# Spectral convolution in a graph layer: complex products combined when they leave the bank, and an inverse transform on full tiles of 128 rows

## The chip, the core and the metric

The kernel runs on one core of one Trainium2 chip. The metric is the device time of one execution in microseconds. In the profile PE is TensorE (matmuls), PEld its weight loads, DVE is VectorE, ACT is ScalarE, POOL is GpSimd and SP is SyncE, which issues transfers. All data is fp32.

## What is computed

One layer of a graph network on 32 sequences of 512 tokens with 256 channels. Cut to what matters:

```python
h = relu(layernorm(x))                                  # (32, 512, 256)
xc = transpose(h)                                       # channels first
c = relu(bn1(conv1d(xc, conv1_w, pad=0)))               # 1 tap
c = bn2(conv1d(c, conv2_w, pad=8))                      # 17 taps, 256 -> 256 channels
x_conv = transpose(relu(c + xc))
s = h @ w_se.T + b_se                                   # 3 features a token
A = exp(-squared_distances(s)) * adj                    # (512, 512) for each sequence
x_nmp = A @ relu(h @ w_msg.T + b_msg)
gi = concat(x_conv, x_nmp) @ w_ih.T + b_ih              # gates of a GRU cell
gh = h @ w_hh.T + b_hh
r, z = sigmoid(gi_r + gh_r), sigmoid(gi_z + gh_z)
out = x + (1 - z) * tanh(gi_n + r * gh_n) + z * h
```

## The kernel before

The 17-tap convolution is done by a discrete Fourier transform. A sequence is cut into 8 pieces of 64 tokens; each piece and the taps are transformed at length 80, which gives 40 units: unit 0 holds the two real frequencies, the units 1 to 39 one complex frequency each. In each unit the spectra of 128 pieces (16 sequences, one half of the batch) are multiplied with the 256 x 256 weights of that frequency. A complex product is put together from three real ones (re and im are the spectra, wr and wi the weights):

- k1 = re (wr + wi)
- k2 = (re + im) wi
- k3 = (im - re) wr
- real part = k1 - k2, imaginary part = k1 + k3

The kernel before never forms the last line. It writes k1, k2 and k3, and the inverse transform has three rows per unit whose coefficients hold the sums. So a piece of tokens has 3 x 40 = 120 rows.

The stages, in order of time: transform of the first 16 sequences, and of the taps (up to about 165 us); "nodes", the aggregation A @ messages, with the products of the first half between (to about 455); transform of the second half, with the last products of the first half and sums of gate weights between (to about 590); nodes and products of the second half (to about 890); then the gates, two sequences (a "pair") at a time, each pair with its inverse transform (to the end).

```python
UNITS = L // 2                                 # L = 80, V = 64 tokens in a piece
ROWS = 3 * UNITS
...
back[3::3], back[4::3], back[5::3] = 2 * (cos - sin).T, -2 * cos.T, -2 * sin.T
...
def product(pw, g, u, xf):                     # half g of the batch, unit u
    ...
    y = pw.tile([P, 3, D], FP, tag="y", name=f"y_{g}_{u}", bufs=3)
    p = bank(f"py_{g}_{u}")                    # one of 8 PSUM banks, in turn
    if u == 0:
        terms = [(p[:, :D], re, wr), (p[:, D : 2 * D], im, wi)]
    else:
        both, wsum = BOTH.pop((g, u)), WSUM.pop((g, u))
        p2 = bank(f"py2_{g}_{u}")
        terms = [(p2[:, :D], both[:, 1], wr), (p[:, D : 2 * D], both[:, 0], wi), (p[:, :D], re, wsum)]
    for dst, v, w in terms:
        for ic in range(DC):
            nc.tensor.matmul(dst, v[:, ic, :], w[:, ic, :], start=(ic == 0), stop=(ic == DC - 1))     # L381
    for k in range(2):
        nc.scalar.copy(by_half(y[:, k, :]), halves(p[:, k * D : (k + 1) * D]))                        # L383
    if u == 0:
        nc.vector.memset(y[:, 2, :], 0.0)
    else:
        nc.vector.tensor_copy(by_half(y[:, 2, :]), halves(p2[:, :D]))                                 # L387
    nc.scalar.dma_start(YD[g][:, 3 * u : 3 * u + 3, :], y)                                            # L388
...
def combine_weights():                         # sums of gate weights, between the second half's transforms
    for k, src in enumerate((w_hhT, w_ihT[D:], w_ihT[:D])):
        w, t = (pools["sums"].tile([P, n, 3 * P], FP, tag=f"w{n}", ...) for n in (4, 7))   # one buffer each
        ...                                    # load w; 4 steps on GpSimd and ScalarE (L825), then write t out
...
def load_pair(p, queue=nc.sync):
    yt = [pools["ops"].tile([ROWS, W // 2, D], FP, tag="yt", ..., bufs=5) for k in range(4)]
    ...
    queue.dma_start(t, YD[g][w : w + W // 2].rearrange("w r d -> r w d"))                             # L535
...
def inverse(p):                                # W = 8 pieces, DC = 2 halves of the channels
    CP[p] = pools["ops"].tile([P, 7, N], FP, tag="cp", name=f"cp_{p}")
    for j in range(2):
        for oc in range(DC):
            bk = bank(f"pc2_{2 * p + j}_{oc}")
            for w in range(W):
                t0, t1 = max(0, w * V - PAD), min(N, w * V - PAD + L)
                u0 = t0 - (w * V - PAD)
                nc.tensor.matmul(bk[:, t0:t1], YT[p][j * W + w][:, oc * P : (oc + 1) * P],
                                 back[:, u0 : u0 + t1 - t0], start=(w == 0), stop=(w == W - 1), ...)  # L572
            xc = CP[p][:, 2 * oc + j, :]
            nc.vector.scalar_tensor_tensor(xc, bk, scale2[:, oc : oc + 1], HP[p][:, 2 * oc + j, :],
                                           op0=ALU.mult, op1=ALU.add)                                 # L575
            nc.scalar.activation(xc, xc, AF.Relu, bias=shift2[:, oc : oc + 1], scale=1.0)             # L577
...
for p in range(pairs):                         # the last stage
    ...
    gates_rz(p, terms, between)                # PE pg, L583
    inverse(p + 1)                             # PE pc, L572
    sums(CP[p + 1], False)                     # GpSimd, L561: four differences of the seven operands
    gate_n(p, terms, False)                    # PE pn, L583
```

The gates multiply 2 x 2 blocks with seven products in place of eight, so each operand (HP, NP, CP) has four blocks and differences of them. In the transform stages a sequence needs: statistics on VectorE (L282, L284, L287), 1/std on GpSimd (L288), normalising on VectorE (L294), transposes on TensorE (phT, L305), the 1-tap convolution (pc, L318) and the transform (px, L333).

Of the kernel before, what the change touches and what calls it, by code (L numbers as in the profile page):

```python
# [11 lines left out]
FP = mybir.dt.float32  # L12
# [3 lines left out]
P = 128  # L16
# [11 lines left out]
ROWS = 3 * UNITS  # L28
WROWS = 2 * UNITS


def dft_constants(taps):

    u = np.arange(L)[:, None]
    f = np.arange(1, UNITS)[None, :]
    cos, sin = np.cos(2 * np.pi * u * f / L), np.sin(2 * np.pi * u * f / L)
    alt = (1.0 - 2.0 * (np.arange(L) % 2))[:, None]
    spectrum = np.zeros((L, L))
    spectrum[:, :1], spectrum[:, 1:2] = 1.0, alt
    spectrum[:, 2::2], spectrum[:, 3::2] = cos, -sin  # L40
    forward = np.zeros((2 * V, 2 * L))
    forward[:V, :L] = forward[V:, L:] = spectrum[:V]
    weights = np.zeros((L, WROWS))
    weights[:, :1], weights[:, 1:2] = 1.0, alt
    weights[:, 2::2], weights[:, 3::2] = cos, -sin

    back = np.zeros((ROWS, L))
    back[0], back[1] = 1.0, alt[:, 0]
    back[3::3], back[4::3], back[5::3] = 2 * (cos - sin).T, -2 * cos.T, -2 * sin.T

    groups = np.zeros((P, WROWS))
    for q in range(4):
        groups[32 * q : 32 * q + taps] = weights[:taps][::-1]
    return [a.astype(np.float32) for a in (forward, groups, back / L)]
# [3 lines left out]
def gnn_layer(  # L58
# [59 lines left out]
    fwd_np, taps_np, back_np = dft_constants(KT)  # L118
# [4 lines left out]
    w1_in = early.tile([P, DC, D], FP, name="w1_in")  # L123
    load_rows(w1_in, w1T, nc.scalar)
    fwd = early.tile([P, 2 * L], FP, name="fwd")
    nc.scalar.dma_start(fwd, nc.inline_tensor(fwd_np, name="dft_fwd").ap())
    taps = early.tile([P, WROWS], FP, name="taps")
    nc.scalar.dma_start(taps, nc.inline_tensor(taps_np, name="dft_taps").ap())
    back = consts.tile([ROWS, L], FP, name="back")
# [43 lines left out]
    batch_norm("bn1", scale1, shift1, nc.gpsimd)  # L173
# [4 lines left out]
    setup = ExitStack()  # L178
    pools["setup"] = setup.enter_context(tc.tile_pool(name="setup", bufs=2))
    ones = pools["setup"].tile([P, P], FP, name="ones", bufs=1)  # L180
    nc.vector.memset(ones, 1.0)

    def bn1_row(i, v):
        for c in range(DC):
            diag = pools["setup"].tile([P, P], FP, tag="diag", name=f"diag_{i}_{c}")
            nc.scalar.activation(diag, ident, AF.Copy, scale=v[:, c : c + 1])
            nc.tensor.matmul(row1[i][:, c * P : (c + 1) * P], ones, diag, start=True, stop=True)

    def scale_w1():
        for c in range(DC):  # L190
            nc.vector.tensor_mul(w1[:, c, :].rearrange("p (i q) -> p i q", i=DC), by_parity(w1_in[:, c, :]),
                                 by_parity(row1[0][:, :D]))
# [3 lines left out]

    bn1_row(0, scale1)
    bn1_row(1, shift1)
    setup.close()

# [24 lines left out]
    WD = dram.tile([WROWS, D * D + 4 * D], FP, name="wd")  # L225
# [18 lines left out]
    def weights_to_freq(gen, pc, i):  # L244

        per = N // D
        s = i % SI
        if s == 0:
            for q in range(4):
                WST[q] = gen.tile([WROWS, SI, D], FP, tag="wst", name=f"wst_{pc}_{i}_{q}", bufs=8)  # L250
        ps = []
        for q in range(4):
            p = bank(f"pw_{pc}_{i}_{q}")
            nc.tensor.matmul(p[:WROWS, :], taps[32 * q : 32 * q + KT, :],  # L254
                             W2P[pc][32 * q : 32 * q + KT, i : i + per, :], start=True, stop=True)
            ps.append(p)
        for q in range(4):
            dst = WST[q][:, s : s + per, :]
            src = ps[q][:WROWS, :].rearrange("r (i d) -> r i d", d=D)
            if q == 3 or (q == 1 and s == 0):  # L260
                nc.vector.tensor_copy(dst, src)
            else:
                nc.scalar.copy(dst, src)
        if s + per == SI:
            for q in range(4):
                i0 = QI * q + PI * pc + i + per - SI
                nc.sync.dma_start(WD[:, i0 * D : (i0 + SI) * D], WST[q].rearrange("r i d -> r (i d)"))

# [96 lines left out]
    def product(pw, g, u, xf):  # L365
        if u > 0 and (g, u) not in BOTH or (g, u) not in WT:
            prepare(pw, g, u, xf)
        wt = WT.pop((g, u))
        re, im = factors_of(xf, u)
        wr, wi = wt[:, 0], wt[:, 1]  # L370
        y = pw.tile([P, 3, D], FP, tag="y", name=f"y_{g}_{u}", bufs=3)
        p = bank(f"py_{g}_{u}")
        if u == 0:
            terms = [(p[:, :D], re, wr), (p[:, D : 2 * D], im, wi)]
        else:
            both, wsum = BOTH.pop((g, u)), WSUM.pop((g, u))
            p2 = bank(f"py2_{g}_{u}")
            terms = [(p2[:, :D], both[:, 1], wr), (p[:, D : 2 * D], both[:, 0], wi), (p[:, :D], re, wsum)]
        for dst, v, w in terms:
            for ic in range(DC):  # L380
                nc.tensor.matmul(dst, v[:, ic, :], w[:, ic, :], start=(ic == 0), stop=(ic == DC - 1))  # L381
        for k in range(2):
            nc.scalar.copy(by_half(y[:, k, :]), halves(p[:, k * D : (k + 1) * D]))  # L383
        if u == 0:
            nc.vector.memset(y[:, 2, :], 0.0)
        else:
            nc.vector.tensor_copy(by_half(y[:, 2, :]), halves(p2[:, :D]))  # L387
        nc.scalar.dma_start(YD[g][:, 3 * u : 3 * u + 3, :], y)  # L388
# [104 lines left out]
    def combine_weights():  # L493

        steps = []
        for k, src in enumerate((w_hhT, w_ihT[D:], w_ihT[:D])):
            w, t = (pools["sums"].tile([P, n, 3 * P], FP, tag=f"w{n}", name=f"w{n}_{k}") for n in (4, 7))
# [25 lines left out]
    def load_pair(p, queue=nc.sync):  # L523
        yt = [pools["ops"].tile([ROWS, W // 2, D], FP, tag="yt", name=f"yt_{p}_{k}", bufs=5) for k in range(4)]
        HP[p] = pools["ops"].tile([P, 8, N], FP, tag="hp", name=f"hp_{p}")
        NP[p] = pools["ops"].tile([P, 7, N], FP, tag="np", name=f"np_{p}")
        YT[p] = []
        for j in range(2):
            b = 2 * p + j
            queue.dma_start(HP[p][:, j:4:2], HD[b])  # L530
            g, w0 = b // GB, (b % GB) * W
            for k in range(2):
                t = yt[2 * j + k]
                w = w0 + k * (W // 2)
                queue.dma_start(t, YD[g][w : w + W // 2].rearrange("w r d -> r w d"))  # L535
                YT[p] += [t[:, i, :] for i in range(W // 2)]
# [26 lines left out]
    def inverse(p):  # L563

        CP[p] = pools["ops"].tile([P, 7, N], FP, tag="cp", name=f"cp_{p}")
        for j in range(2):
            for oc in range(DC):
                bk = bank(f"pc2_{2 * p + j}_{oc}")
                for w in range(W):
                    t0, t1 = max(0, w * V - PAD), min(N, w * V - PAD + L)  # L570
                    u0 = t0 - (w * V - PAD)
                    nc.tensor.matmul(bk[:, t0:t1], YT[p][j * W + w][:, oc * P : (oc + 1) * P], back[:, u0 : u0 + t1 - t0],  # L572
                                     start=(w == 0), stop=(w == W - 1), skip_group_check=True)
# [203 lines left out]
    def first_part(g, freq, between, left=()):  # L777
# [3 lines left out]
        for b in range(b0, b0 + 3):  # L781
            if b not in X:
                load_x(b, nc.gpsimd if g else nc.sync)
# [59 lines left out]
    with tc.tile_pool(name="freq", bufs=1) as fpool:  # L843
# [3 lines left out]
        with phase("first", "gen"):  # L847
            gen = pools["gen"]
            per = N // D
            steps = [partial(weights_to_freq, gen, pc, i) for pc in range(QI // PI) for i in range(0, PI, per)]  # L850
            load_x(0)
# [68 lines left out]


# [88 lines left out]
```

## Time and profile before

| | |
|---|---|
| time | 1888.97 us, median of 3 (1886.87 to 1891.18) |
| span of the profiled execution | 1883.5 us |
| matmul records of the inverse transform (L572) | 1024, in 16 groups of 64 |
| granted TensorE clock, mean | 0.994 |
| transfers | 309.89 MB, mean 165 GB/s |
| write of a unit's products (yd) | 80 times 384 KB |
| read of a part of a sequence's products (yt) | 480 KB, four per pair |

An fp32 matmul stands in the trace as two records (a pass each). A row of the groups reads: line, engine, operation, what is written from what, shape and count; then busy time in us and the mean of one in ns; then the idle time of the engine ahead of them and what ended it. The mean of one matmul record is longer than the spacing of two, as matmuls overlap; what a matmul costs in a stream is read from a stretch without gaps, divided by its records. The chain of waits gives, followed back from the end, what each moment of the span was spent on.

### The profile page before, as it was taken

The page shows a single profiled execution, that of the slowest core. Times are in us where ns is not written, and L with a number is a line of the kernel's source. Part 1 is how long each engine was busy: PE and PEld are TensorE (multiplying, and loading weights), DVE is VectorE, ACT ScalarE, POOL GpSimd, SP SyncE. Part 2 cuts the span into 40 slices and gives each one's busy share as a digit, 9 for nine tenths or more (in the row PEclk, how much of TensorE's full clock was granted, in tenths as well). Part 3 has the DMA queues.
Part 4 walks back from the last instruction along what each step waited for, and adds up shares of the span by engine and source line. Part 5 has one row for each costly group of instructions (what it writes and reads, how often), then busy time and mean ns, then how long its engine had stood idle before and what let it go on. Part 6 is the DMA issues. An engine that isn't in the chain of part 4 may idle for free.

```text
span 1883.5 us, 20947 instructions
## 1 busy us (share of the span) xinstructions
PE 1844.1 (98%) x6982; PEld 1110.4 (59%) x6982; DVE 1084.0 (58%) x2162; ACT 599.9 (32%) x1153; POOL 583.1 (31%) x565
## 2 busy tenths in 40 slices
PE   7999999999999999999999999999999999999997
PEld 5677666665888676665545554555445554555453
DVE  7775554544986445444266456654665456645666
ACT  3545443432335444343212221222212221222121
POOL 3331343434432344445321332133222322133220
PEclk9999999999999999999999999999999999999999
DMA  7999998776568997878542455235532554245512
GB/s 217 292 273 236 252 265 250 217 221 208 173 235 206 263 273 240 249 226 230 146 103 57 104 132 131 59 73 131 132 81 53 129 132 106 55 102 131 131 28 40
DMA packets 316537, 309.89 MB, mean 165 GB/s; under 512 B 148631, under 2 KB 245815, under 8 KB 316047
## 3 DMA queue, kind: packets, MB, share of 16 engines
q1 hardware_dynamic: 289727, 232.09, 48.4%
q10 hardware_dynamic: 19024, 49.17, 7.2%
q0 software_dynamic: 7680, 27.30, 5.3%
q8 instruction: 56, 0.92, 0.2%
q14 instruction: 50, 0.41, 0.1%
HBM read 201.60 MB, written 106.89 MB: 164 GB/s over the span
## 4 chain that ended last, share of the span: by engine, by line
PE 91%; issue 2%; DVE 2%; DMA 2%; POOL 1%; ACT 1%; SPq 0%; POOLq 0%; ACTq 0%; DVEq 0%
PE pg L583 29%; PE pn L583 14%; PE pn L474 11%; PE py L381 11%; PE pc L572 6%; PE pm L425 6%; PE pc L318 5%; PE px L333 3%; PE pw L254 2%; PE pd L460 2%; PE phT L305 1%; PE psr L449 1%; DMA hT<-hd 1%; DVE stats L282 0%; PE pz L583 0%
## 5 line engine op out<-in xcount | busy, mean ns | idle before, releaser
L561 POOL TENSOR_TENSOR hp<-hp 128x512 f32<-128x512 f32 x64 | 94.8, 1491 | 467.2 <-DMA hp<-hd 366.9
L474 PE MATMUL pn<-A,msg 128*128 128x512 f32 x512 | 225.0, 592 | 0.0
L583 PE MATMUL pg<-hp,sw 128*128 128x512 f32 x434 | 221.9, 593 | 0.7 <-DVE rz L602 0.5
L583 PE MATMUL pg<-cp,sw 128*128 128x512 f32 x434 | 221.6, 592 | 0.0
L583 PE MATMUL pg<-np,sw 128*128 128x512 f32 x434 | 221.6, 592 | 0.0
L474 PEld LDWEIGHTS pn<-A,msg 128*128 128x128 f32 x512 | 97.1, 190 | 110.6 <-issue 107.7
L362 POOL TENSOR_TENSOR both<-xf 128x256 f32<-128x256 f32 x78 | 60.3, 773 | 321.4 <-PE py L381 288.7
L381 PE MATMUL py<-wt,both 128*128 128x256 f32 x624 | 150.4, 384 | 0.7 <-issue 0.7
L598 ACT ACTIVATE rz<-rz,brz 128x512 f32<-128x512 f32 x93 | 67.0, 721 | 260.2 <-DVE rz L602 260.2
L583 PEld LDWEIGHTS pg<-hp,sw 128*128 128x128 f32 x434 | 82.2, 190 | 104.8 <-issue 97.6
L583 PEld LDWEIGHTS pg<-cp,sw 128*128 128x128 f32 x434 | 82.5, 190 | 103.8 <-issue 103.8
L583 PEld LDWEIGHTS pg<-np,sw 128*128 128x128 f32 x434 | 82.5, 190 | 103.8 <-issue 103.8
L381 PEld LDWEIGHTS py<-wt,both 128*128 128x128 f32 x624 | 114.1, 190 | 43.4 <-issue 26.5
L466 DVE TENSOR_TENSOR A<-e,at 128x512 f32<-128x512 f32 x128 | 111.5, 910 | 41.7 <-ACT e L463 41.6
L561 POOL TENSOR_TENSOR cp<-cp 128x512 f32<-128x512 f32 x64 | 80.5, 1268 | 177.2 <-ACT cp L577 176.0
L349 POOL TENSOR_TENSOR wsum<-wt 128x512 f32<-128x512 f32 x78 | 108.1, 1386 | 52.3 <-DMA wt<-wd 46.8
L318 PE MATMUL pc<-w,hT 128*128 128x256 f32 x512 | 120.2, 389 | 1.5 <-DVE hT L306 1.5
L572 PEld LDWEIGHTS pc<-back,yt 120*128 120x128 f32 x1024 | 116.9, 192 | 7.7 <-issue 7.7
L702 ACT ACTIVATE nt<-nt,vech 128x512 f32<-128x512 f32 x64 | 46.2, 722 | 233.9 <-DVE nt L701 233.9
L425 PE MATMUL pm<-wmsg,hq 128*128 128x259 f32 x512 | 117.6, 381 | 1.3 <-ACT hq L411 1.3
L387 DVE COPY y<-py 128x256 f32<-128x256 f32 x78 | 32.7, 419 | 147.4 <-PE py L381 147.4
L572 PE MATMUL pc<-back,yt 120*128 120x80 f32 (+1 forms) x1024 | 116.2, 274 | 0.0
(136 smaller groups left out, 2969.9 us busy)
## 6 DMA issues: line engine op xcount, KB each, us to landing
wt<-wd SPq DMA_DIRECT2D x160, 256.0 KB, 4.7
adj<-in_adj_dram SPq DMA_DIRECT2D x128, 256.0 KB, 6.4
yd<-y ACTq DMA_DIRECT2D x80, 384.0 KB, 5.2
yt<-yd SPq DMA_DIRECT2D x60, 480.0 KB, 8.3
wd<-wst SPq DMA_DIRECT2D x64, 320.0 KB, 5.1
hd<-hT SPq DMA_DIRECT2D x32, 512.0 KB, 4.4
nd<-nmp ACTq DMA_DIRECT2D x32, 512.0 KB, 4.1
xb<-in_x_dram SPq DMA_DIRECT2D x128, 128.0 KB, 3.3
```

The source lines that it names most:

```text
L318: nc.tensor.matmul(p[:, j, :], HT[b][:, ic, c * P : (c + 1) * P], w1[:, ic, :], start=(ic == 0), stop=(ic == DC - 1))
L333: nc.tensor.matmul(p[:, j * 2 * L : (j + 1) * 2 * L], H1[b][:, c0 + j, ic * P : (ic + 1) * P], fwd, start=True, stop=True)
L349: nc.gpsimd.tensor_tensor(t, WT[g, u][:, 0], WT[g, u][:, 1], op=ALU.add)
L362: nc.gpsimd.tensor_tensor(both[:, 0], re, im, op=ALU.add)
L381: nc.tensor.matmul(dst, v[:, ic, :], w[:, ic, :], start=(ic == 0), stop=(ic == DC - 1))
L425: nc.tensor.matmul(p[:, : D + NS], hq[:, ic, c * P : (c + 1) * P], wmsg[:, ic, :], start=(ic == 0), stop=(ic == DC - 1))
L466: nc.vector.tensor_mul(A[b][:, mc, :], e, at)
L474: nc.tensor.matmul(p, MSG[b][:, mc, dc * P : (dc + 1) * P], A[b][:, mc, :], start=(mc == 0), stop=(mc == NC - 1))
L561: nc.gpsimd.tensor_tensor(t[:, dst, :], t[:, a, :], t[:, b, :], op=sub)
L572: nc.tensor.matmul(bk[:, t0:t1], YT[p][j * W + w][:, oc * P : (oc + 1) * P], back[:, u0 : u0 + t1 - t0], start=(w == 0), stop=(w == W - 1) ...
L583: nc.tensor.matmul(bk[:, t], sw[:, k, q, o, :], terms[k][q][:, t], start=(first and i == 0), stop=(i == len(ks) - 1), skip_group_check=True)
L598: nc.scalar.activation(rz[:, g, j, :], src, AF.Sigmoid, bias=brz[:, g : g + 1], scale=1.0)
```

## The change

The complex products are completed when they leave PSUM: ScalarE copies k1, VectorE subtracts k2 and adds k3. So a unit has two rows in place of three, a piece of tokens 80 rows in place of 120, and the 8 pieces of a sequence 640 rows, which fill 5 tiles of 128 rows without a rest. A tile then spans parts of two or three pieces. Its inverse transform is one matmul with a table of its own that reaches over the tokens of all pieces it touches: 136, 208, 144, 208 and 136 columns. Its purpose is fewer matmuls in the inverse transform and fewer bytes written and read.

Along with it go changes of buffers: the operand yt has two tiles per pair and four buffers; the sums of gate weights get a second buffer for the result (w7); the weights of the 1-tap convolution are loaded into a buffer that is used later anyway, and last in ScalarE's queue; and the batch-norm rows are computed at the start of the first stage in a borrowed buffer, ahead of the first sequence's statistics.

```diff
-ROWS = 3 * UNITS
+ROWS = 2 * UNITS
...
-    back[3::3], back[4::3], back[5::3] = 2 * (cos - sin).T, -2 * cos.T, -2 * sin.T
+    back[2::2], back[3::2] = 2 * cos.T, -2 * sin.T
+    rows = np.zeros((tokens // V * ROWS, tokens + L))
+    for w in range(tokens // V):
+        rows[w * ROWS : (w + 1) * ROWS, w * V : w * V + L] = back / L
+    rows = rows[:, taps // 2 :]
+    pieces, spans = [], []
+    for r in range(0, len(rows), P):
+        first, last = r // ROWS, (r + P - 1) // ROWS
+        spans.append((max(0, first * V - taps // 2), min(tokens, last * V - taps // 2 + L)))
+        pieces.append(rows[r : r + P, slice(*spans[-1])])
... (product)
-        for k in range(2):
-            nc.scalar.copy(by_half(y[:, k, :]), halves(p[:, k * D : (k + 1) * D]))
-            nc.vector.tensor_copy(by_half(y[:, 2, :]), halves(p2[:, :D]))
-        nc.scalar.dma_start(YD[g][:, 3 * u : 3 * u + 3, :], y)
+            nc.scalar.copy(y_im, halves(k1))
+            nc.vector.tensor_sub(y_re, y_im, halves(k2))
+            nc.vector.tensor_add(y_im, y_im, halves(k3))
+        nc.scalar.dma_start(YD[g][:, 2 * u : 2 * u + 2, :], y)
... (combine_weights)
-            w, t = (pools["sums"].tile([P, n, 3 * P], FP, tag=f"w{n}", name=f"w{n}_{k}") for n in (4, 7))
+            w, t = (pools["sums"].tile([P, n, 3 * P], FP, tag=f"w{n}", name=f"w{n}_{k}", bufs=m) for n, m in ((4, 1), (7, 2)))
... (load_pair)
-        yt = [pools["ops"].tile([ROWS, W // 2, D], FP, tag="yt", name=f"yt_{p}_{k}", bufs=5) for k in range(4)]
+        YT[p] = [pools["ops"].tile([P, len(spans), D], FP, tag="yt", name=f"yt_{p}_{j}", bufs=4) for j in range(2)]
...
-                queue.dma_start(t, YD[g][w : w + W // 2].rearrange("w r d -> r w d"))
+            rows = YD[g][w0 : w0 + W].rearrange("w r d -> (w r) d")
+            queue.dma_start(YT[p][j], rows.rearrange("(c p) d -> p c d", p=P))
... (inverse)
-                for w in range(W):
-                    t0, t1 = max(0, w * V - PAD), min(N, w * V - PAD + L)
-                    u0 = t0 - (w * V - PAD)
-                    nc.tensor.matmul(bk[:, t0:t1], YT[p][j * W + w][:, oc * P : (oc + 1) * P], back[:, u0 : u0 + t1 - t0],
-                                     start=(w == 0), stop=(w == W - 1), skip_group_check=True)
+                for c, (t0, t1) in enumerate(spans):
+                    nc.tensor.matmul(bk[:, t0:t1], YT[p][j][:, c, oc * P : (oc + 1) * P], back[:, n : n + t1 - t0],
+                                     start=(c == 0), stop=(c == len(spans) - 1), skip_group_check=True)
+                    n += t1 - t0
... (beginning of the first stage)
-    batch_norm("bn1", scale1, shift1, nc.gpsimd)
-    bn1_row(0, scale1)
-    bn1_row(1, shift1)
+        if g == 0:
+            t = XN[b0] = pools["first"].tile([P, NC, D], FP, tag="xn", name="rows", bufs=2)
+            ones, diags = t[:, 0, :P], t[:, 1:3, :].rearrange("p i (c m) -> p i c m", m=P)
+            nc.vector.memset(ones, 1.0)
+            batch_norm("bn1", scale1, shift1, nc.gpsimd)
+            bn1_row(0, scale1, ones, diags)
+            bn1_row(1, shift1, ones, diags)
```

## The prediction, made before the changed kernel had run

> **What bounds the kernel now.** I read the busy times first, then the chain that ended last by line, then that chain in order of time. The first two, from the profile page:
>
> ```profile
> PE 1844.1 (98%) x6982; PEld 1110.4 (59%) x6982; DVE 1084.0 (58%) x2162; ACT 599.9 (32%) x1153; POOL 583.1 (31%) x565
> PE 91%; issue 2%; DVE 2%; DMA 2%; POOL 1%; ACT 1%; SPq 0%; POOLq 0%; ACTq 0%; DVEq 0%
> PE pg L583 29%; PE pn L583 14%; PE pn L474 11%; PE py L381 11%; PE pc L572 6%; PE pm L425 6%; PE pc L318 5%; PE px L333 3%; PE pw L254 2%; PE pd L460 2%; PE phT L305 1%; PE psr L449 1%; DMA hT<-hd 1%; DVE stats L282 0%; PE pz L583 0%
> ```
>
> TensorE sets the end almost everywhere. So a TensorE microsecond saved is a microsecond of the kernel, while work moved between the other engines counts only where it delays TensorE. The part that the change makes shorter on TensorE is the inverse transform, L572, 6% of the span. The chain in order of time shows one pair of sequences in the last stage, and then three pieces of the stage that transforms the second half:
>
> ```profile
> 933.65 7.10 PE pc L572 x64
> 940.75 18.07 PE pn L583 x42
> 958.83 36.05 PE pg L583 x84
> ...
> 575.39 0.87 PE phT L305 x8
> 576.26 3.46 PE pc L318 x16
> 579.72 2.17 PE px L333 x16
> ```
>
> The columns are start, duration, and what ran how often. The three pieces of a pair follow each other without a gap: 7.10 + 18.07 + 36.05 = 61.22 us, sixteen times. An fp32 matmul appears as two records. Dividing each duration by its count gives the spacing of records: 512 columns (L583) take 36.05/84 = 429 ns, 256 columns (L318) 216 ns, 160 columns (L333) 136 ns, 128 columns (L305) 109 ns, and the 72 or 80 columns of L572 7.10/64 = 111 ns. From 512 and 256 columns: 213 ns for 256 more columns, so 0.832 ns a column plus 3 ns; for 160 that gives 136 ns, as measured. For 80 it would give 70 ns, but 111 is measured, the same as for 128. The inverse is therefore limited by something that doesn't depend on the columns.
>
> **What the Trainium skill says.** "TensorE: Matmul & The Clock Gate", section "LDWEIGHTS (loading the stationary operand)", puts a weight load at its number of columns divided by 1.2, in ns, independent of the rows. For 128 columns that is an estimate of 107 ns; the trace agrees with 111 ns between records of L572, whose two groups on the page are
>
> ```profile
> L572 PEld LDWEIGHTS pc<-back,yt 120*128 120x128 f32 x1024 | 116.9, 192 | 7.7 <-issue 7.7
> L572 PE MATMUL pc<-back,yt 120*128 120x80 f32 (+1 forms) x1024 | 116.2, 274 | 0.0
> ```
>
> Loads are busy for all of the matmuls' time here: L572 is load-bound, so fewer and wider matmuls are the right medicine. For the combining of products, "VectorE: DVE Perf Modes", section "Why PSUM operands drop a tier", says that an fp32 operation with an operand in PSUM gets no faster mode. The trace agrees in that a copy from the bank (L387) and an addition with one operand in the bank (L428) cost alike for 256 elements:
>
> ```profile
> L383 ACT COPY y<-py 128x256 f32<-128x256 f32 x160 | 51.7, 376 | 83.1 <-PE py L381 82.9
> L387 DVE COPY y<-py 128x256 f32<-128x256 f32 x78 | 32.7, 419 | 147.4 <-PE py L381 147.4
> L428 DVE TENSOR_TENSOR msg<-pm,bmsg 128x256 f32<-128x256 f32 x128 | 52.9, 414 | 0.1
> ```
>
> **The change, part by part.**
>
> *Inverse transform.* Per sequence and half of the channels there were 8 matmuls, 16 records of 111 ns: 1776 ns. Now there are 5, over 136, 208, 144, 208 and 136 columns (sum 832 against 624 before). By 0.832 a column plus 3 ns: 116, 176, 123, 176, 116, together 707 ns a pass and 1415 ns for both passes. All five are above the 111 ns of a load, so loads no longer limit. A pair has four such banks: 5.66 us for 7.10, a saving of 1.44 us, times 16 pairs = **23.0 us**. All of it lies on the path. Does something else then end last? VectorE's eviction (L575, mean 750 ns) fits into 1415 ns. After the last bank come 750 ns on VectorE, 722 on ScalarE (L577) and one difference on GpSimd (1268), some 2.9 us with the hand-overs; the first matmul that needs that difference is the sixth of the next gate, five matmuls or 10 x 429 = 4.3 us after the bank. The same 1.4 us of slack as before. Loading 1280 KB a pair from YD in place of 1920 KB only helps.
>
> *Products.* TensorE does the same 12 records per unit, in the same order in both built programs. ScalarE loses one copy a unit, 78 x 376 ns = 29 us; VectorE gets two operations of about 415 ns for one copy: 78 x 415 = 32 us more, to some 59% of the span. In the stages with products, the window 200 to 440 us has TensorE busy for 238.9 of 240 us and VectorE for 123.8; 610 to 860 has 250.0 and 120.0. About 14 us more for VectorE in each stays far from the bound. Both banks of a unit are held about 1.2 us longer (copy, difference and sum behind the last product); the pool hands a bank out again eight allocations later, and among the next eight there is always a message block (3.5 us) or an aggregation (6.9 us). Gain or loss: **0**. Only at the start of the second half's transform, where TensorE waits for VectorE's normalising, may the additions cost 0.5 us.
>
> *Weight sums.* The buffer for the seven combinations of gate weights (w7) is doubled. Before, GpSimd could not begin the next matrix until the 1344 KB of the last one had been written out:
>
> ```profile
> 541.40 0.99 POOL L825 TENSOR_TENSOR w<-w,w 128x384 f32<-128x384 f32 x1
> 544.68 0.81 SPq L825 DMA_DIRECT2D ws<-w  x1
> 556.35 0.99 POOL L825 TENSOR_TENSOR w<-w 128x384 f32<-128x384 f32 x1 [8.59 <-issue]
> 558.10 1.04 POOL L288 TENSOR_TENSOR rstd<-rstd,minus_half 128x4 f32<-128x4 f32 x1
> 559.18 2.13 DVE L294 TENSOR_SCALAR xn<-x,mv,rstd 128x256 f32<-128x256 f32 x4 [5.12 <-POOL rstd L288]
> 560.41 2.28 PE L305 MATMUL phT<-ident,xn 128*128 128x128 f32 x8 [1.89 <-DVE xn L294]
> ```
>
> GpSimd sat for 8.6 us, the next sequence's 1/std stood behind it in its queue, and VectorE and TensorE waited for that. A sequence in this stage takes TensorE 6.50 us (0.87 + 3.46 + 2.17). The convolution of one starts at 551.22, of the next at 562.48 and then 569.59: 11.26 and 7.11 us, 5.4 us too much. With a second buffer the wait for the write goes, but the next gate matrix still has to be loaded into its single buffer; that load is issued between 542.4 and 544.2 and such loads took a median 7.7 us to land, so until about 552. The next 1/std is due at about 552.6. I count **4.8 us** saved of 5.4.
>
> *Beginning.* The batch-norm chain on GpSimd no longer queues behind the first 1/std, so its four matmuls leave the way of the first transposes (they ended at 14.2 us; about 3 us sooner is possible). But the load of the convolution weights is now last in ScalarE's queue; it took up to 7.2 us to land and VectorE needs it early. I count **0** plus or minus 1.5 us. The transform table grows from 38 to 426 KB once, beside a DMA share of 0.9 in that stage: at most 1 us, counted as 0.
>
> *Sum.* 1888.97 - 23.0 - 4.8 + 0.5 = 1861.7 us, 1.4% less.
>
> **The rivals.**
> 1. *Width is not free: the accumulating matmuls over 208 overlapping columns cost more than the line through other shapes says, or the first load of each is not hidden.* For it: L572 itself doesn't lie on that line. Against: L333 (160 columns) does, with a new weight for each matmul as well. If each record cost 176 ns, ten records would take 1760 ns, and the inverse would save nothing: 1884 us.
> 2. *The products' new chain becomes a wait.* VectorE works its instructions off in order; a difference that waits for ScalarE's copy holds up the multiplications that make A (L466), and TensorE waits for A. For it: the chain across ScalarE is new and VectorE is half busy. Against: A is made one sequence ahead, and in the waits of TensorE's weight loads A appears once, with 0.4 us. If it cost 0.3 us in each of 30 sequences: 9 us, 1871 us.
> 3. *The buffer gains nothing, because the single load buffer replaces the wait by another of the same length.* Then 1866 to 1867 us.
> 4. *More is won:* the beginning gives 1.5 us, the whole 5.4 us return, no product delays: 1859 us or a little under.
>
> **Range and chances.** The inverse is arithmetic on measured spacings, with an error of perhaps 2 us. Weight sums and beginning together add about 3 us either way, rival 2 mostly upwards. I predict 1862 us, 8 times in 10 between 1855 and 1870. Faster by over 2% would need less than 1851.2 us, 10.5 us beyond my sum: 0.05. Slower by over 2% needs a wait of over 60 us that nothing in the trace prepares: 0.01. The rest, 0.94, is within 2%.
>
> **What would show it.** Right: 40 records per pair at the inverse in about 5.66 us (mean spacing 141 ns) and a pair of 59.8 us; the sequence at 551 us without the 5 us gap on TensorE; VectorE about 32 us busier, ScalarE 29 us less busy, with nothing changed in the stages of the products (about 20 us a sequence in the second). Wrong: a spacing near 176 ns at the inverse, TensorE waiting for y, A or a bank in the stages with products, GpSimd still waiting some 8 us at the third gate matrix, or a beginning that is longer than before. Any of these moves the time as its rival says.

## The result and the profile after

The changed kernel takes 1865.5 us (median of 4 runs, 1861.68 to 1868.29), the kernel before 1887.9 us beside it (1884.74 to 1891.18). The ratio is 0.988, with a 95% interval from 0.9854 to 0.9905. The profiled execution has a span of 1859.9 us; before it was 1883.5 us. The same views as before, from the page of the changed kernel: busy time of each engine, then the shares of the chain that ended last, by engine and by line.

```profile
PE 1821.4 (98%) x6598; PEld 1086.5 (58%) x6598; DVE 1111.7 (60%) x2238; ACT 577.8 (31%) x1075; POOL 579.2 (31%) x563
PE 90%; issue 3%; DMA 2%; DVE 2%; POOL 2%; ACT 1%; SPq 0%; ACTq 0%; POOLq 0%; DVEq 0%
PE pg L585 29%; PE pn L585 15%; PE py L385 10%; PE pn L480 10%; PE pc L320 6%; PE pm L431 6%; PE pc L573 5%; PE px L335 4%; PE pw L256 2%; PE pd L466 2%; PE phT L307 1%; DMA sw<-ws 1%; PE psr L455 1%; PE pz L585 1%; DMA hT<-hd 1%
```

TensorE has 384 records and 22.7 us less, and its share is the same 98%: what it lost in work is nearly all that the span lost (23.6 us). VectorE is 27.7 us busier, ScalarE 22.1 us less busy; neither comes near the bound. Transfers fell from 309.89 to 289.25 MB; what that alone is worth was not tested, and in the pairs, below, nothing is left over for it. The new entry for `sw<-ws` is a load that the chain happens to follow at the first gate; TensorE waited 0.3 us for it.

The chain in order of time, one pair of the last stage:

```profile
1051.40 5.65 PE pc L573 x40
1057.05 18.02 PE pn L585 x42
1075.08 36.05 PE pg L585 x84
1111.12 5.65 PE pc L573 x40
```

The inverse is 40 records in 5.65 us, 141 ns apart, and again there is no gap on either side. A pair takes 59.72 us where it took 61.22.

To see where the 23.6 us of the two spans came from, I divided both at the same events: the first message matmul of each half, the first gate matmul and the last stage's first `pz` matmul.

| stretch | before, us | after, us | difference |
|---|---|---|---|
| start to the first message matmul | 169.7 | 170.6 | +0.9 |
| from there to the first message matmul of the second half | 419.8 | 417.2 | -2.6 |
| from there to the first gate (with the first pair's inverse) | 307.9 | 307.4 | -0.5 |
| the pairs, 15 inverses | 955.7 | 933.7 | -22.0 |
| the end | 30.4 | 31.0 | +0.6 |

Fifteen times 1.45 us is 21.8 us: the pairs give back the inverse and nothing else. The second stretch holds several things at once; the next views show two of them. GpSimd's timeline at the third gate matrix:

```profile
542.91 0.99 POOL L834 TENSOR_TENSOR w<-w,w 128x384 f32<-128x384 f32 x1
543.85 0.84 POOL L118 DMA_DIRECT2D x<-in_x_dram  x1
548.25 1.03 POOL L290 TENSOR_TENSOR rstd<-rstd,minus_half 128x4 f32<-128x4 f32 x1 [3.56 <-DVE rstd L289]
551.58 1.00 POOL L834 TENSOR_TENSOR w<-w 128x384 f32<-128x384 f32 x1 [2.31 <-DMA hd<-hT]
```

GpSimd starts the third matrix after 2.3 us of idle time where it had been 8.6, and 1/std is no longer behind it. The convolutions of this stretch start at 542.03, 548.54, 555.04 and 561.54 in the chain, 6.50 us apart each time: the 11.26 and 7.11 us of before are gone, 5.4 us saved. Of these, 0.6 us is the convolution behind the wait, which took 4.23 us in place of 3.62: the granted clock was at half there, from 560.3 to 563.7 us.

So 5.4 us came out of this stretch, but only 2.6 stayed. The chain at the start of the second half's transform shows part of what went back in:

```profile
475.34 5.48 PE pc L320 x16
480.82 2.60 PE py L385 x12
...
483.44 0.38 ACT y L391
...
483.85 0.43 DVE y L392
...
484.30 0.42 DVE y L393
484.72 1.31 DVE stats L284 x4
...
487.75 0.42 DVE xn L296
```

Read it downwards: all twelve records of a product, ScalarE's copy, VectorE's difference and sum, and only then the statistics of the next sequence, which is to be normalised and transposed before TensorE can go on. The way from a finished product to the next transposes now leads across two engines. In the kernel before, VectorE's timeline at the same place reads

```profile
480.28 0.43 DVE L387 COPY y<-py 128x256 f32<-128x256 f32 x1 [0.23 <-PE py L381]
480.62 1.39 DVE L282 BATCH_NORM_STATS2 stats<-x 128x6 f32<-128x256 f32 x4
```

There the product's records began at 479.16, and the statistics 1.46 us later: VectorE's one copy was of the third product, whose matmuls come first. In the changed kernel the records begin at 480.65 and the statistics at 484.64, 3.99 us later. From the first convolution to the third, this stage took 13.1 + 6.5 us before and takes 14.5 + 6.5 us now. These steps hold the first convolution too, which runs partly at half clock (6.36 us before, 5.48 now, 3.62 at full clock). A measure without it is the time from the first record of this product to the next convolution: 6.93 us before (479.16 to 486.09) and 9.20 us now (480.65 to 489.85), so the new chain costs 2.27 us. The product ahead of it costs something as well: from its last record to the first convolution it was 7.55 us, and is 8.02.

### The profile page after: what moved, and what is told of

Same layout as the page of the kernel before. It is cut to its first block, busy times and chain, and to the rows that moved or that the text cites. A ratio compares the mean times of both kernels' runs of the same rounds, so it can differ in the third digit from the quotient of the medians.

```text
span 1859.9 us, 20076 instructions
## 1 busy us (share of the span) xinstructions
PE 1821.4 (98%) x6598; PEld 1086.5 (58%) x6598; DVE 1111.7 (60%) x2238; ACT 577.8 (31%) x1075; POOL 579.2 (31%) x563
## 2 busy tenths in 40 slices
DMA packets 306299, 289.25 MB, mean 156 GB/s; under 512 B 148028, under 2 KB 235612, under 8 KB 305812
## 4 chain that ended last, share of the span: by engine, by line
PE 90%; issue 3%; DMA 2%; DVE 2%; POOL 2%; ACT 1%; SPq 0%; ACTq 0%; POOLq 0%; DVEq 0%
PE pg L585 29%; PE pn L585 15%; PE py L385 10%; PE pn L480 10%; PE pc L320 6%; PE pm L431 6%; PE pc L573 5%; PE px L335 4%; PE pw L256 2%; PE pd L466 2%; PE phT L307 1%; DMA sw<-ws 1%; PE psr L455 1%; PE pz L585 1%; DMA hT<-hd 1%
## 5 line engine op out<-in xcount | busy, mean ns | idle before, releaser
L563 POOL TENSOR_TENSOR hp<-hp 128x512 f32<-128x512 f32 x64 | 80.5, 1269 | 411.4 <-DMA hp<-hd 292.4
L392 DVE TENSOR_TENSOR y<-y,py 128x256 f32<-128x256 f32 x78 | 31.8, 408 | 192.7 <-ACT y L391 187.7
L585 PE MATMUL pn<-hp,sw 128*128 128x512 f32 x224 | 114.4, 592 | 0.0
L585 PE MATMUL pn<-np,sw 128*128 128x512 f32 x224 | 114.4, 592 | 0.0
```

The costliest lines, as they stand in the source:

```text
L563: nc.gpsimd.tensor_tensor(t[:, dst, :], t[:, a, :], t[:, b, :], op=sub)
L585: nc.tensor.matmul(bk[:, t], sw[:, k, q, o, :], terms[k][q][:, t], start=(first and i == 0), stop=(i == len(ks) - 1), skip_group_check=True)
```

## The experiments

Each theory below is about one term of the prediction's sum. "Steps" are the times between the starts of consecutive convolutions.

### What the second buffer for w7 is worth

The changed kernel, with one buffer for the sums of gate weights, as before:

```diff
-..., bufs=m) for n, m in ((4, 1), (7, 2)))
+..., bufs=m) for n, m in ((4, 1), (7, 1)))
```

> The changed kernel with one buffer again for the combined gate weights (w7). Theory of the prediction: the wait of GpSimd for the 1344 KB write comes back at the third gate matrix, and the sequence there takes some 11.3 us in place of 6.50; the stage that transforms the second half ends about 5.5 us later than in the changed kernel, the span is about 1865 us for 1859.9. Rival (the second buffer brought nothing, the stage was shortened by lighter transfers): the stage stays as in the changed kernel, no sequence over 7 us, span 1860 us.

Measured: 1871.33 us (1869.54 to 1873.87), ratio to the kernel before 0.9907 [0.9885, 0.9929]. The wait is back in GpSimd's timeline:

```profile
563.45 0.99 POOL L834 TENSOR_TENSOR w<-w 128x384 f32<-128x384 f32 x1 [7.09 <-issue]
```

The steps here are 9.7 and 7.5 us for 6.5 and 6.5, an excess of 4.2 us (1.0 us of it the convolution behind the wait, 4.59 us long). By medians the buffer is worth 5.1 to 5.8 us (against 1866.22 and 1865.5 us for the changed kernel); the intervals of the ratios overlap, and it is the timeline that shows the cause. Rival 3, that another wait would take its place, is refuted: with two buffers no step in this stretch is longer than 6.50 us.

### What limits the inverse

Two kernels test whether the columns set the time. The first is the kernel before, where each of the 8 matmuls of a bank writes only its piece's own 64 tokens; the 8 tokens on either side, which overlap the neighbours, are left out:

```diff
-                t0, t1 = max(0, w * V - PAD), min(N, w * V - PAD + L)
+                t0, t1 = w * V, (w + 1) * V
```

> The kernel before, with each of the 8 matmuls of the inverse writing only its own 64 tokens in place of 72 or 80; it leaves out what a piece adds to its neighbours. If weight loads set the spacing in the kernel before: a pair's inverse stays at 7.10 us (111 ns a record) and the span at 1883.5 us. If the cost goes by columns, 64 x 0.832 + 3 = 56 ns a record gives 3.6 us a pair, and even a cost in proportion (64/78) gives 5.8 us; then the span falls by 20 to 55 us.

The second is the changed kernel with 5 tiles of 104 columns (96 for the last) side by side; what a tile adds to the tokens beyond these is left out:

```diff
-                for c, (t0, t1) in enumerate(spans):
+                for c, (t0, t1) in enumerate((104 * i, min(N, 104 * i + 104)) for i in range(5)):
```

> The changed kernel with each of its 5 tiles written to 104 columns only (96 for the last), so that every token is still written once; it leaves out most of the sums over tiles. If the changed inverse is bound by columns down to the floor of a load: 40 records at the floor of 111 ns, 4.4 us a pair for 5.65, span 16 x 1.2 = 19 to 20 us shorter, about 1840 us. If columns alone count (no floor): 104 x 0.832 + 3 = 90 ns, 3.6 us a pair, 33 us shorter. If something other than columns and loads sets 141 ns a record, such as full 128 rows or overlapping sums: 5.65 us a pair, no change.

The chain's piece of the inverse, in the kernel before with 64 columns:

```profile
1065.32 7.09 PE pc L572 x64
```

and in the changed kernel with 104 columns:

```profile
1053.05 4.44 PE pc L573 x40
```

7.09/64 and 4.44/40 are both 111 ns. Fewer columns brought nothing before (7.10 us), so a floor of 111 ns a record is shown, whatever the width and whether the tile has 120 or 128 rows. By an estimate from the line of the prediction (0.832 ns a column plus 3 ns) it holds up to 130 columns. That the weight loads make this floor is argued: all weights of the inverse have 128 columns, and no run changed that. Rival 1, that overlapping columns cost more than the line through the other shapes, is refuted by the 5.65 us of the change itself. The second kernel took 1847.96 us in its one execution. 16 times 1.21 us under the medians of the changed kernel would be 1846.1 to 1846.9; the 1840 us expected was counted from the shortest of its executions.

The first kernel took 1895.06 us, 6 us more than the kernel before beside it, though it did less. That isn't its edit: the excess lies in steps ahead of the gates (in one sequence of the nodes ScalarE waited 5.38 us for the landing of hT, and at the third gate matrix the steps were 11.8 and 8.6 us). A single time says little here: seven executions of the kernel before, taken beside it, spread from 1884.67 to 1893.82 us. The lines of the trace repeat to 0.01 us (7.10 and 7.09).

### Whether ScalarE's copy holds up the nodes

In the stages with the nodes, the steps of the changed kernel are the 17.4 and 20.0 us of before, but for two that are 0.9 us longer. To see whether the new chain across ScalarE does that, VectorE makes the copy itself:

```diff
-            nc.scalar.copy(y_im, halves(k1))
+            nc.vector.tensor_copy(y_im, halves(k1))
```

> The changed kernel with VectorE copying k1 itself, so that the difference waits for TensorE only, and no longer for ScalarE's queue; one more VectorE operation a unit. Theory (VectorE's queue is held up because ScalarE's copy stands behind a copy of hq that waits for a transfer): the two places in the stages with products where TensorE lost 0.9 us each (at about 240 and 642 us) go back to the rhythm of the kernel before, though VectorE is 30 us busier; the start of the second half's transform stays slow or gets slower by some 0.4 us a product; the span is 1 to 2 us shorter than 1859.9. Rival (it is VectorE's load itself): it gets worse by 1 us or more in the stages with products.

Measured: 1866.19 us (1863.23 to 1868.54), ratio 0.9873 [0.9846, 0.9901]; no difference from the changed kernel. VectorE is busy for 1144.0 us in place of 1111.7, at no cost that shows in the total. At the start of the second half's transform it takes 9.59 us from the product to the convolution, where 9.20 were measured with ScalarE's copy; but the 104-column kernel, with ScalarE's copy, takes 9.61 as well, so the 0.4 us expected there isn't shown. Single long steps remain (1.7 us in the first half, 1.5 in the second) and end on a transfer; ScalarE's timeline:

```profile
646.79 0.62 ACT L417 COPY hq<-hT 128x512 f32<-128x512 f32 x1 [5.84 <-DMA hT<-hd]
```

So the copy isn't what lengthens them. In the step shown a late landing of hT does, and the 64-column version of the kernel before shows the same. Why it lands late in some executions and not in others was not settled. In the ten profiles with the changed code the long steps of these stages add up to 1.4 to 5.8 us, in the two of the kernel before to 0 and 5.5 us; whether the change has a part in them stays open.

### Where the gain of the weight sums went

The next four ran beside each other. The first is the changed kernel once more, to compare with:

> The changed kernel once more, as the yardstick of this group: the stages seen so far in four profiles with its code of the beginning put the third convolution of the first stage at 36.5 to 39.6 us, against 36.0 and 36.4 with the old beginning, and the step from the first to the second convolution of the second half's stage at 14.5 to 15.2 us, against 13.1 and 13.4. If these are properties of the change and not chance, they show again: 36.5 to 40 us, and 14.5 us or more. Time about 1865 us.

Measured: 1866.22 us (1861.99 to 1869.53), ratio 0.9891 [0.987, 0.9911], span 1860.2 us. The two steps at the start of the second half's transform were 15.2 and 8.2 us this time, 3.8 us more than before the change. From the product to the next convolution it is 9.20 us, as in the first profile. What is longer is that convolution itself; in the chain, first in the profile of the result, then in this one:

```profile
490.02 3.46 PE pc L320 x16
489.58 5.14 PE pc L320 x16
```

From 490 to 493 us the granted clock was 1.00 in the first and 0.51 in the second. This half clock came in five of the seven profiles in which TensorE waits for the combination (second steps of 7.8 to 8.2 us), and in none of the five in which it doesn't (the kernel before, whole and with 64 columns, and the three versions with the later combination below).

The second splits a product into its matmuls and its leaving of the bank. Only at the start of the second half's transform, for the first two products, copy, difference and sum are put into the queues behind the next sequence's statistics and transposes:

```diff
... (product, with one more argument, later=None; units other than 0)
+        def leave():
             nc.scalar.copy(y_im, halves(k1))
             nc.vector.tensor_sub(y_re, y_im, halves(k2))
             nc.vector.tensor_add(y_im, y_im, halves(k3))
             nc.scalar.dma_start(YD[g][:, 2 * u : 2 * u + 2, :], y)
+        if later is None: leave()
+        else: later.append(leave)
...
-    left = [[partial(prepare, pw, 0, u1, xf), partial(product, pw, 0, u0, xf)],
-            [partial(prepare, pw, 0, u2, xf)],
-            [partial(product, pw, 0, u1, xf)],
-            [partial(product, pw, 0, u2, xf)]]
+    left = [[partial(prepare, pw, 0, u1, xf), partial(product, pw, 0, u0, xf, later)],
+            [leave, partial(prepare, pw, 0, u2, xf)],
+            [partial(product, pw, 0, u1, xf, later)],
+            [leave, partial(product, pw, 0, u2, xf)]]
```

> The changed kernel, but at the start of the second half's transform the copy, difference and sum of the first two products are queued behind the statistics and transposes of the next sequence. Theory (in that stretch VectorE sets the pace, its two operations a product stand in front of the statistics, and it waits for ScalarE's copy of a product that isn't finished): the wait of about 2.3 us on VectorE for ScalarE's copy goes, the step from the first to the second convolution falls from 14.5 to 15.2 us to some 13 us or less, and a second step over 6.5 us doesn't follow; span 1.5 to 3.5 us shorter than the changed kernel's. Rival (the landing of x or GpSimd's queue sets the pace there): no change.

Measured: 1859.63 us (1858.81 to 1860.38), ratio 0.985 [0.9834, 0.9865], 6.6 us under the changed kernel. The steps are 13.0 and 6.5 us, as in the kernel before; from the product to the convolution it is 6.93 us again, and ahead of the first convolution 7.23 us in place of 8.02. The chain at this place is TensorE alone:

```profile
482.22 2.59 PE py L385 x12
484.81 0.87 PE phT L307 x8
485.68 2.59 PE py L385 x12
488.28 0.87 PE phT L307 x8
489.15 3.46 PE pc L320 x16
```

Products, transposes and convolution follow each other without VectorE or ScalarE between them, where the chain of the changed kernel went through L391, L392, L393 and the statistics. It is shown that the place of the combination in VectorE's queue costs this stage 3.1 us (2.27 + 0.79), and 1.3 to 1.7 us more where the next convolution falls into the half clock. Against the unedited kernel's profile that is 4.8 of the 6.6 us by which the medians differ; the rest is not shown to come from the edit. The change of the study also issues the second half's first three loads of x at an earlier place in the program; this kernel keeps that and still returns to 6.93 us, so the loads aren't what cost the time. (The two profiled executions differ by 1.7 us only: the beginning was 1.8 us longer in the edited one.)

A third kernel asked which part of that queue it is. It is the changed kernel with the products in another order on TensorE, so that the one that ScalarE copies is finished first:

```diff
-    terms = [(k3, both[:, 1], wr), (k2, both[:, 0], wi), (k1, re, wsum)]
+    terms = [(k1, re, wsum), (k2, both[:, 0], wi), (k3, both[:, 1], wr)]
```

> The changed kernel with the three products of a unit in the order k1, k2, k3 on TensorE, so that the one that ScalarE copies is finished first. If VectorE is held up by the way across ScalarE (the copy of the last product, some 0.4 to 0.8 us each time), both steps of the second half's start get back most of the loss: 13.0 to 13.5 and 6.5 us in place of 15.2 and 8.2, total 1860 to 1862 us. If it is held up because the combination stands ahead of the statistics while the products aren't finished at all, only 0.8 us per product comes back: steps of 14 to 14.7 and 7.4 to 8 us, total 1864 to 1866 us.

Measured: 1868.95 us (1866.32 to 1870.52), ratio 0.9879 [0.9854, 0.9903]; steps of 14.7 and 6.5 us. The total is no better than that of the changed kernel, where 1860 to 1866 us were expected; its profile has 5.8 us of long steps in the stages with nodes. The statistics now start 3.20 us after the product's first record (488.18 after 484.98) in place of 3.99, and from the product to the convolution it is 8.40 us in place of 9.20: the 0.8 us of the second theory, out of 2.27. The first theory, in which the copy alone does it, falls. What holds VectorE is that the difference and the sum stand ahead of the statistics and need nearly the whole product; the copy only adds to it. The second step of 6.5 us, which the second theory put at 7.4 to 8, tells nothing: it hangs on the clock, and the unedited kernel shows both 6.5 and 8.2.

### The beginning

In nine profiles the third convolution of the first stage starts at

| kernel | us |
|---|---|
| before; before with 64 columns | 36.0; 36.4 |
| changed, twice | 36.5; 36.5 |
| changed, with one edit elsewhere (104 columns, one w7 buffer, VectorE copies, combination later, copied product first) | 39.6; 39.6; 39.2; 38.3; 38.3 |

so the new beginning loses 0.5 to 3.6 us. One theory was that the transform tables, which ScalarE's queue now loads ahead of the convolution weights, push back the taps of the first weights. The test puts the old order back:

```diff
-    nc.scalar.dma_start(fwd, ...)              # ahead of w_in
-    nc.scalar.dma_start(taps, ...)
...
     load_w1()
+    nc.scalar.dma_start(fwd, ...)
+    nc.scalar.dma_start(taps, ...)
```

> The changed kernel, but the weights of the 1-tap convolution are loaded ahead of the two transform tables again, as in the kernel before. Theory (with the new order the first load of taps waits for the landing of the vectors[...]; TensorE then stands idle for the taps and runs at a lower clock afterwards): the loads of taps are issued at 1.8 us in place of 3.2 to 4.7, the wait of TensorE for them (2.1 to 3.0 us) is 1 us or less, the third convolution starts at about 35 us, span 1.5 to 3 us shorter. Rival (the taps land late because the transfers share the bandwidth): they land as late as before, no gain.

Measured: 1868.72 us (1865.48 to 1872.99), ratio 0.9899 [0.9876, 0.9923]. The theory fell: the first of the taps' loads was issued at 1.8 us (3.2 in the changed kernel), as expected, but the last at 9.6 (7.9), and the taps' transform began only at 13.58, the first convolution at 17.23 and the third at 38.3 us. What the timelines of TensorE have in common is something else. The changed kernel, and below it the first convolution of the kernel before:

```profile
8.72 1.92 PE L307 MATMUL phT<-ident,xn 128*128 128x128 f32 x8
13.04 2.09 PE L256 MATMUL pw<-w2p,taps 17*80 17x512 f32 x16 [2.40 <-DMA w2p<-in_w2T_dram]
15.06 5.24 PE L320 MATMUL pc<-w,hT 128*128 128x256 f32 x16
...
16.29 3.72 PE L318 MATMUL pc<-w,hT 128*128 128x256 f32 x16
```

The batch-norm rows and the transposes were moved forward, but TensorE's queue then holds the taps' transform, and the taps are there only at 13.0 us (TensorE came to them at 14.3 us in the kernel before, and didn't wait). TensorE idles for 2.40 us, and then works more slowly: the convolution takes 5.24 us, before 3.72. The windows from 13 to 20 us of the changed kernel have the granted clock ahead of the DMA share and the GB/s:

```profile
13.00:15.00 2.00, 1.96 (x16) 0.65 (x16) 2.00 (x6) 0.87 (x2) 2.00 (x4) 0.94 0.56 219
15.00:20.00 5.00, 5.00 (x20) 4.13 (x17) 2.25 (x4) 2.25 (x5) 1.80 (x4) 0.68 0.92 202
```

It was granted 0.68 of full speed in the 5 us in which the kernel before had 1.00. In finer windows it is half the clock, from 14.8 to 18.2 us, and about as long in the other execution of this kernel. In the five kernels with an edit elsewhere the half clock begins at 13.3 to 15.2 us and lasts 6.8 us: that sets the last row of the table apart, not its edits. The Trainium skill, "TensorE: Matmul & The Clock Gate", section "What's actually happening", says that the clock is throttled by default and released by activity, and that an idle window of about 3.4 us throttles it. The direction agrees with the trace, but the idle times here, 1.83 to 3.03 us, are shorter than the page's figure. Nor do they decide how long it lasts: 2.40 us was followed by 3.4 us of half clock in the changed kernel, 2.39 us by 6.8 us in the one with the later combination. That the idle time is the cause is likely, not shown.

If the wait is the loss, TensorE needs other work while it waits for the taps. Two kernels give it some: in the first stage, the transposes of the first sequence are queued before the second one's statistics, and its convolution before the taps' transform. Both keep the later combination; the first also keeps the old order of loads.

```diff
+            if g == 0:
+                transpose_h(b0)
             ...                                # statistics and normalising of b0 + 1
-            transpose_h(b0)
+            if g:
+                transpose_h(b0)
...
+                conv1(b)                       # ahead of the taps' transform
...
-                conv1(b)
```

> Both edits together, and at the very beginning the first sequence is transposed and convolved ahead of the second one's statistics and of the taps' transform, so that TensorE has work while the taps are on their way. If the gains add up: 3 to 5 us less than the changed kernel, near 1861 us median, with the third convolution of the first stage at 34 to 35 us. If the beginning is set by the landing of the third x alone, the reordering adds nothing to the two edits.

Measured: 1855.33 us (1854.74 to 1857.08), ratio 0.9829 [0.9813, 0.9845]. The first convolution starts at 11.27 us, the third at 35.05.

> The later combination and the first stage's new order on TensorE (first sequence's transposes before the second's statistics, its convolution before the taps' transform) without the old order of the loads. If the order on TensorE makes the difference between 1859.6 and 1855.3 us (the gap until the taps land is filled): 1855 to 1857 us, the third convolution of the first stage at 35 to 36 us. If the order of the loads makes it: 1859 to 1860 us, the third convolution at about 38 us. The convolution weights are loaded last here, so a middle result is possible if the first convolution must wait for them.

Measured: 1858.84 us (1854.77 to 1862.89), ratio 0.983 [0.9804, 0.9855]. Its timeline of TensorE:

```profile
9.08 1.92 PE L307 MATMUL phT<-ident,xn 128*128 128x128 f32 x8
11.43 4.35 PE L320 MATMUL pc<-w,hT 128*128 128x256 f32 x16 [0.44 <-DVE hT L308]
15.71 3.16 PE L256 MATMUL pw<-w2p,taps 17*80 17x512 f32 x16
```

The 2.40 us of idle time are 0.44, and the third convolution starts at 34.7 us. The place in the stage is as the first theory said, with or without the old order of loads; the order of the work on TensorE makes the gain of the beginning. The half clock is not gone: it comes at 19.6 us here and at 20.4 us in the other, for 6.8 us in both, but until 23 us TensorE then waits for the second sequence anyway. The totals of the two can't be told apart by their intervals, nor can that of the second, 1858.84 us where 1855 to 1857 were expected, from the later combination alone (1859.63); the 2.9 us between their spans arise after the transform of the second half, in the stages that both have alike. By medians these are the fastest complete versions, about 11 and 7 us under the changed kernel.

## Why the prediction was right, step by step

- **Inverse, 23.0 us saved: right.** 16 times 1.45 us, 23.2 us, from 0.832 ns a column plus 3 ns and the floor of a record. The 107 ns that the prediction estimated for a load stands at 111 ns a record in three kernels; the floor is shown, its cause argued.
- **Weight sums, 4.8 of 5.4 us: right, a little too careful.** The steps lost the whole 5.4 us, 0.6 us of it through the clock, and taking the buffer away cost 5.1 to 5.8 us. The load into the single buffer, for which 0.6 us was held back, ended no wait of TensorE.
- **Products in the stages with nodes, 0: not contradicted.** Two long steps cost 1.9 us in the profile of the result, and it stays open whether the change has a part in them. TensorE was busy for 239.0 of 240 us between 200 and 440 us, 249.9 of 250 between 610 and 860. Making VectorE 32 us busier still didn't change the total.
- **Start of the second half's transform, 0.5 us lost: mis-sized.** The combination costs 2.27 us at one product and about 0.5 at the one ahead of it, and 1.3 to 1.7 us more where the clock falls behind the wait. The prediction counted the additions, not the wait ahead of them. It is the mechanism of rival 2, an in-order VectorE that holds up what TensorE waits for, but in the stage where statistics are next in the queue, not in the one where A is. There the work that TensorE waits for is made a sequence ahead, as was said; here it isn't.
- **Beginning, 0 plus or minus 1.5 us: too good.** It lost 0.5 to 3.6 us. That the batch-norm chain leaves the way of the transposes was right; that TensorE would have to wait for the taps in any case, and be granted half of its clock after it, was not seen. The suspected load of the convolution weights was not the cause.
- **VectorE 32 us busier, ScalarE 29 less: the sizes were 27.7 and 22.1 us.** The difference against a bank took 408 ns, the sum 420 (415 was counted), the copies of ScalarE that remain a mean of 371 ns.

In the profiled executions the terms nearly close: -23.2 for the inverse, -5.4 for the weight sums, +0.9 up to the first message matmul, +1.9 for long steps of the nodes, +1.9 at the start of the second half (0.5 + 1.4), +0.6 at the end give -23.3 of the -23.6 us between the spans. The sum of the prediction, 1861.7 us, is 3.8 us below the measured median, and 4.9 below if it starts from the 1887.9 us measured beside the changed kernel. The two big terms were even 0.8 us too small, so what is missing are costs in places where it counted 0.5 us together: a wait in VectorE's queue, a wait for the taps, the half clock behind both, and perhaps the long steps. That the fastest of the four executions, 1861.68 us, meets the sum is luck.

## What to carry to other kernels

Before making a matmul narrower, divide its stretch by its records: where that gives the same figure as for a wider one, the columns don't set the time, and fewer, wider matmuls can pay even when they compute more: here 832 columns in 5 matmuls took less than 624 in 8. When work moves into an engine's queue, don't ask how busy the engine is but what stands behind the new instruction and who waits for it; the same pair of instructions showed no clear cost in the stages of the nodes and cost some 3 us in the one place where statistics stood behind it. A wait of TensorE can cost more than its length, as the clock may be at half after it. And work that is moved forward on an engine gains nothing if the next entry of its queue waits for a transfer: look for something that can fill the gap.

## What the runs showed of the hardware

- The floor of 111 ns a record was the same for 64, for 72 or 80, and for 104 columns (7.09/64, 7.10/64 and 4.44/40 us), with 120 and with 128 rows.
- An idle time of 2.40 us on TensorE, early in the kernel, was followed by 3.4 us at half the clock: 16 records of 256 columns took 5.24 us, in the kernel before 3.72. So 1.5 us were lost behind the gap as well. In other executions of the same beginning the half clock lasted 6.8 us.
- Even an idle time of 1.44 us (ahead of the transposes at 487.88 us in the repeat of the changed kernel) was followed by half the clock, from 489.5 to 492.9 us. In the profile of the result 1.43 us at the same place was not: the same program runs at either clock there.
- The column of the granted clock can miss a slow stretch: with the old order of loads it reads 1.00 from 13 to 23 us, though the convolution at 17.23 us took 5.02 us in place of 3.72.
- Taps whose loads were issued earlier were not there earlier: with the first at 1.8 us in place of 3.2, the last was issued at 9.6 us in place of 7.9, and TensorE used them only from 13.6 us (13.0).
